# Layer 0's early fetches of the expert sums go out two per block over five blocks, and the last plan's pieces follow each other one step apart

## The chip, the cores and the metric

The kernel runs on one core of one Trainium2 chip. A time is the device time of one execution in microseconds (us), and lower is better. Times are medians over timed executions; the profile comes from one more execution, which has its own time. TensorE (PE) does matmuls, VectorE (DVE) and ScalarE (ACT) elementwise work, GpSimd (POOL) elementwise work and the indirect DMAs, SyncE (SP) only issues DMAs.

## What is computed

Two layers work on 2708 rows of 256 floats. Each layer adds to `x` first an attention over the rows that a 2708 x 2708 matrix `adj` allows, and then a mixture of experts (8 experts of width 1024 in layer 0, 16 of width 512 in layer 1), where each row goes to the two experts that its gate prefers. Cut from the reference:

```python
x = x + _L0_gnn_ref(_layernorm(x), adj, L0_gnn_W, L0_gnn_a)
x = x + _L0_ffn_ref(_layernorm(x)[None], Wg, bg, W1, b1, W2, b2)[0]
x = x + _L1_gnn_ref(_layernorm(x), adj, 1, W_gcn, W_att, a_att)
x = x + _L1_ffn_ref(_layernorm(x)[None], gate_w, gate_b, w1, b1, w2, b2, gamma, beta)[0]

# _L0_ffn_ref, the part that the change lies in
top_w, top_i = jax.lax.top_k(xf @ Wg + bg, 2)
top_w = jax.nn.softmax(top_w, axis=-1)
for e in range(E):
    h = jax.nn.gelu(xf @ W1[e] + b1[e], approximate=False)
    out = out + w_dense[:, e:e + 1] * (h @ W2[e] + b2[e])
```

## The kernel before

The rows lie in 22 tiles of 128 (two at the end are shorter), taken in 11 pairs. Layer 0's attention runs pair by pair. When a pair's attention is closed (`close0`, L1357), its rows are normalized, gated, ranked by expert and scattered by GpSimd into a table in device memory, `rows_d`, that is cut into blocks of 128 rows, each block of one expert. Layer 0's experts then run over 47 blocks in `Experts.run` (L1191), and with them layer 1 begins: its first step is to read the sums and to project them.

**One block.** For block b, TensorE does 32 matmuls for the hidden layer (L972), 2 for the turn of the next block's rows (L515), and then 1 + 16 matmuls for the outputs of block b - 1 (L987, L990). ScalarE evicts the hidden layer in eight pieces (L976, `ht`) and the turned rows (L957, `xt`). VectorE scales the outputs (L996, `yo`), and GpSimd adds them with an indirect DMA into one of two arrays in device memory, `sums0[0]` for even and `sums0[1]` for odd blocks (L1001). An add waits until the add before it on the same array has landed.

**What SyncE issues.** Its program for block b is: the first weights of block b + 2 (L834, 1 MB), the second weights of block b + 2 (L838, 1 MB, after the outputs of block b - 1, whose room they take), the rows of block b + 3 (L850, 130 KB), and then what `beside(b)` adds. Weights have three rooms. SyncE's queue is in order, so that a DMA stands behind all that were issued ahead of it.

**The early fetches.** `beside` is `combine` (L1584), which calls `ahead(b)` (L1556). Tokens of the first five pairs have all their expert rows in blocks below `DONE` = 32, so their sums are final long before the last block. In block 40 (`left == 6`), `ahead` fetches the sums of pairs 0 to 2, and in block 41 those of pairs 3 and 4: for each pair one DMA of 256 KB from each of the two arrays (`fetch_rows`, L1523 and L1528) into two places of `h_all`. Right behind a pair's fetches, GpSimd adds the two (L1566, 128x512). In blocks 43 and 44 (`left` 3 and 2) VectorE takes statistics of these rows, and in block 45 they are normalized and stored. After the last block, layer 1 goes on with these five pairs, and fetches the other six (`prepare1`, L1635).

**The plan.** Before blocks can run, the kernel must know which expert and which rows each one has. `plan` (L862) computes that with small instructions that go from VectorE to TensorE (`number_ps`, L908), back to VectorE (`at`, `sel`, L912 to L916), to TensorE (`where_ps`, L921), to ScalarE and VectorE (`where`, L925; `hot_f`, L933), to TensorE (`bias_ps`, L943) and to ScalarE (L948). It runs twice: 24 blocks when eight pairs are routed, the other 26 after the last pair, while the first blocks are already computed. Where its pieces stand among the other instructions is set by `Turns`: a piece yields a number of steps, and `in_steps` (L1349) yields `before` ahead of a TensorE piece and `after` behind one. `run` calls `steps(k)` at three places in a block with 2, 1 and 2 steps: after the hidden layer, after the turn, and after the outputs.

```python
for engine, *_ in piece:
    if "PE" in (engine, last):
        yield before if engine == "PE" else after
    last = engine
```

TensorE, ScalarE, VectorE and SyncE run in the order in which the program is written; GpSimd's order is the scheduler's.

Of the kernel before, what the change touches and what calls it, by code (L numbers as in the profile page):

```python
# [17 lines left out]
OP = mybir.AluOpType  # L18
# [41 lines left out]
class Mark:  # L60

    at = None
# [85 lines left out]
def kernel(  # L148
# [25 lines left out]
    nc = tc.nc  # L174

    ctx.enter_context(tc.manual_schedule(engines={ET.PE, ET.Activation, ET.DVE, ET.SP}))
    N, D = x.shape
# [9 lines left out]
    pairs = [tiles[k:k + 2] for k in range(0, T, 2)]  # L187
# [7 lines left out]
    SURE0, SURE1, KEEP, LATE, DEEP, AHEAD1 = 47, 45, 3, 12, 4, 8  # L195
# [56 lines left out]
    h_all = lasting.tile([P, T, D + 1], F32, name="h_all")  # L252
# [10 lines left out]
    def xn_tile():  # L263
        return lasting.tile([P, RW], F32, name="xn", bufs=4)

    def xr0_tile():
        return lasting.tile([P, RW], F32, name="xr", bufs=5)

    def xt_tile():
        return keep0.tile([P, D], F32, name="xt", bufs=3)  # L270
# [11 lines left out]
    def parts_of_rows(r):  # L282

        return [(0, r)] if r == P else [(0, 64), (64, r)]
# [33 lines left out]
    def filled(name, value, cols=1, dtype=F32, pool=const):  # L318
        tl = pool.tile([P, cols], dtype, name=name)
        nc.gpsimd.memset(tl, value)  # L320
        return tl
# [54 lines left out]
    def ts(a, s1, op0, s2=None, op1=None, dtype=F32):  # L376
        o = stat(a.shape[1], dtype)
        if op1 is None:
            nc.vector.tensor_scalar(o, a, s1, None, op0=op0)
        else:  # L380
            nc.vector.tensor_scalar(o, a, s1, s2, op0=op0, op1=op1)
        return o
# [23 lines left out]
    def at_once(steps):  # L406

        while True:
            try:
                next(steps)  # L410
            except StopIteration as end:
                return end.value
# [23 lines left out]
    def rsqrt(v, o=None):  # L436
        return at_once(rsqrt_steps(v, o))
# [88 lines left out]
    minus_one, half, ones_f = filled("minus_one", -1.0), filled("half", 0.5), filled("ones_f", 1.0, 96)  # L526
# [822 lines left out]
    def in_steps(piece, before, after):  # L1349

        last = "DVE"
# [5 lines that stand above are left out]
    def close0(pair, ahead, behind, last=False):  # L1357


        for i, r in pair:  # L1360
            ps = accs.pop(i)
            ri = row.tile([P, 1], F32, name="rinv")
            nc.vector.reciprocal(ri[:r], ps[:r, D:D + 1])
            nc.vector.scalar_tensor_tensor(x_all[:r, i, :], ps[:r, :D], ri[:r], x_all[:r, i, :],
                                           op0=OP.mult, op1=OP.add)
            experts0.store(i, r, x_all[:r, i, :])
            ln_f0.stats(x_all[:r, i, :], i, r)
            yield 1
        if last:
            lo, n = pair[0][0], len(pair)  # L1370
            rsqrt(ts(ln_f0.mv[:, lo:lo + n, 1], LN_EPS, OP.add), ln_f0.rstd[:, lo:lo + n])
        else:
            yield behind - 1
            ln_f0.root(pair)
            yield 1
            ln_f0.mend(pair)
        for t, r in pair:
            router0.rows[t] = xr0_tile()
            ln_f0.apply(router0.rows[t][:r, :D], x_all[:r, t, :], t, r)
            yield 1  # L1380
        yield ahead - 1
        router0.turn(pair)
        yield behind
        router0.evict(pair)
        yield ahead
        router0.gate(pair)
        yield behind
        router0.take(pair)
        at_once(router0.pick(pair, 0))
        yield 1  # L1390
        at_once(router0.pick(pair, 1))
        yield ahead
        router0.rank(pair)
        yield behind
        at_once(router0.number(pair))
        for t, r in pair:
            router0.scatter(t, r)
        if pair is pairs[FULL0]:
            yield from in_steps(experts0.plan(EARLY0), 1, behind)
        if last:  # L1400
            yield from in_steps(experts0.plan(experts0.NB), 1, behind)

    turns = Turns()
    sums0 = []

    FULL0 = 7
    EARLY0 = 2 * (FULL0 + 1) * 2 - E0
    experts0 = Experts(
        0, router0, L0_ffn_W1, L0_ffn_b1, L0_ffn_W2, AF.Gelu, sums0, ("wide", "acc", "mt"),
        lambda b: xn_tile() if b < 4 else late0.tile([P, RW], F32, name="xg", bufs=6),  # L1410
        lambda: xt_tile().rearrange("p (c n) -> p c n", n=P), w0_tile, SURE0)
# [26 lines left out]
    for step in range(START + T * len(pairs)):  # L1438
# [15 lines left out]
        if step >= START:  # L1454
            k, j = divmod(step - START, T)
# [21 lines left out]
    for last in late:  # L1477
        gather(*last)
    nc.scalar.preload_act_table_set(GELU_TABLE)
    turns.start(close0(pairs[-1], 2, 2, True))  # L1480
    turns.step()
    a0_scope.close()
# [40 lines left out]
    def fetch_rows(tl, src, group):  # L1523

        full = [t for t, r in group if r == P]
        if full:
            lo = full[0] * P
            ins = nc.sync.dma_start(tl[:, :len(full)], src[lo:lo + len(full) * P, :].rearrange(  # L1528
                "(t p) d -> p t d", p=P))
        if len(full) < len(group):  # L1530
            for lo, hi in parts_of_rows(TAIL):
                ins = nc.sync.dma_start(tl[lo:hi, len(full):], src[TF * P:W, :].rearrange(
                    "(t p) d -> p t d", p=P)[lo:hi])
        return ins
# [3 lines left out]
    def keep_rows(src, pair):  # L1538
        if pair[1][1] == P:
            lo = pair[0][0] * P  # L1540
            nc.sync.dma_start(x_d[lo:lo + 2 * P, :].rearrange("(t p) d -> p t d", p=P), src)
        else:
            for q, (t, r) in enumerate(pair):
                for lo, hi in parts_of_rows(r):
                    nc.sync.dma_start(x_d[t * P + lo:t * P + hi, :], src[lo:hi, q])
# [4 lines left out]
    AHEAD = 5  # L1550
    MOST, DONE = 4 * AHEAD + E0 - 1, EARLY0 + E0
    normed = {}
    assert AHEAD <= FULL0 + 1 and MOST <= DONE and DONE <= SURE0 - 9
    first, at2 = tiles[:2 * AHEAD], T - 2 * AHEAD

    def ahead(b):  # L1556

        left = SURE0 - 1 - b
        if left in (6, 5):
            for k in range(3) if left == 6 else range(3, AHEAD):  # L1560

                for half, at in ((0, 2 * k), (1, at2 + 2 * k)):
                    experts0.early_read(half, fetch_rows(h_all[:, at:at + 2, :D], sums0[half],
                                                         pairs[k]), DONE)
                xa = h_all[:, 2 * k:2 * k + 2, :D]
                nc.gpsimd.tensor_tensor(xa, xa, h_all[:, at2 + 2 * k:at2 + 2 * k + 2, :D], OP.add)  # L1566
        if left in (3, 2):
            for t, r in first[:6] if left == 3 else first[6:]:
                ln_a1.stats(x_all[:, t], t, r)
        if left == 1:  # L1570
            rsqrt(ts(ln_a1.mv[:, :2 * AHEAD, 1], LN_EPS, OP.add), ln_a1.rstd[:, :2 * AHEAD])
            for k, pair in enumerate(pairs[:AHEAD]):
                keep_rows(h_all[:, 2 * k:2 * k + 2, :D], pair)
                if k < AHEAD - 1:
                    normed[k] = [(xn_tile if k < 2 else xr0_tile)()[:, :D] for _ in pair]
                    for xp, (t, r) in zip(normed[k], pair):
                        ln_a1.apply(xp, x_all[:, t], t, r)

    with tc.tile_pool(name="experts0", bufs=1) as late0:
        room = late0.tile([P, 4096], F32, name="room2")  # L1580
        experts0.add_room(2, room[:, :2048], room[:, 2048:])
        l1_weights = []

        def combine(b):  # L1584
            if b == EARLY0 + 2:
                l1_weights.extend(load_combined(late0))
            if b == EARLY0 + 4:
                combine_weights(*l1_weights)
            ahead(b)

        experts0.run(late0, turns, (2, 1, 2), combine)
# [291 lines left out]
    xr_slots, taken_at, left = {}, {t: Mark() for t in range(0, T, 2)}, {part[0][0]: len(part) for part in parts1}  # L1883
# [617 lines left out]
```

## Time and profile before

| what | us |
|---|---|
| median of 3 timed runs | 1144.73 |
| lowest and highest of them | 1137.87 to 1148.16 |
| the profiled execution | 1135.28 |
| its span, first to last instruction | 1133.6 |
| TensorE busy in the span | 1038.0 (92%) |
| VectorE, ScalarE, GpSimd busy | 542.4, 576.4, 368.5 |
| mean granted TensorE clock | 0.961 |
| layer 0's experts, first hidden matmul to last output matmul | 294.5 to 660.6 |

The profile is read as follows. "L996 DVE ... `yo<-out_ps,w`" is an instruction of line 996 on VectorE that writes the tile `yo` from `out_ps` and `w`. In a timeline, the first two columns are the start in us from the span's start and the time that a run of like instructions takes together; "[1.96 <-DMA room...]" says that the engine stood idle 1.96 us before it and that the landing of that DMA ended the wait. A row of the stretches gives, for a stretch of the span, the busy time of each engine with its instructions, then the granted clock of TensorE, the share of the 16 DMA engines that was busy, and the GB/s that they moved. "SPq" lines are DMAs that SyncE issues, with the time that the issue took.

### The profile page before, as it was taken

To read this page: it belongs to the slowest core of one execution; us is meant where nothing else is said; L and a number is where in the kernel's file an instruction comes from. 1 tells how busy PE (TensorE), PEld (TensorE's weight loads), DVE (VectorE), ACT (ScalarE), POOL (GpSimd) and SP (SyncE) were. 2 spreads that over 40 slices of the span, in tenths; PEclk is the share of its full clock that TensorE was granted. 3 is DMA by queue.
4 is the path that set the end of the run, shared out by engine and by line. 5 is a ranking of instruction groups with operands and counts; after the bars stand their busy time and mean duration, and the time that the engine had idled before them with its cause. 6 is when DMAs were issued, how large, how long until landed. Compare 5 with 4: busy or idle time off the path is not lost. (4 is left out here: it accounts for less than half of the span.)

```text
span 1133.6 us, 21472 instructions
## 1 busy us (share of the span) xinstructions
PE 1038.0 (92%) x6707; PEld 921.6 (81%) x6707; DVE 542.4 (48%) x2210; ACT 576.4 (51%) x1602; POOL 368.5 (33%) x425
## 2 busy tenths in 40 slices
PE   5999999998989999999999999898985967999994
PEld 3788888887879999998999854898984856999882
DVE  7778888887421111101110347577865553122257
ACT  4866667664524444444444346545653633544454
POOL 7531112111242222112213361352534155434350
PEclk9999999999999999999999999997996788999997
DMA  9965454431889999999899959401114656785893
GB/s 289 282 248 177 137 176 152 170 95 55 306 252 283 331 323 321 325 305 319 257 312 331 356 155 279 160 1 51 53 61 130 179 138 144 162 203 105 227 292 129
DMA packets 161862, 234.38 MB, mean 207 GB/s; under 512 B 10891, under 2 KB 137798, under 8 KB 159032
## 3 DMA queue, kind: packets, MB, share of 16 engines
q1 hardware_dynamic: 143356, 209.90, 57.0%
q0 software_dynamic: 18384, 23.03, 10.6%
q8 instruction: 56, 0.92, 0.3%
q14 instruction: 66, 0.54, 0.2%
HBM read 205.54 MB, written 54.59 MB: 229 GB/s over the span
## 5 line engine op out<-in xcount | busy, mean ns | idle before, releaser
L996 DVE TENSOR_SCALAR yo<-out_ps,w 128x256 f32<-128x256 f32 x89 | 43.0, 483 | 383.3 <-PE out_ps L990 376.2
L1346 PE MATMUL att_ps<-g_all,z 128*128 128x257 f32 (+3 forms) x968 | 223.6, 383 | 0.0
L1346 PEld LDWEIGHTS att_ps<-g_all,z 128*128 128x128 f32 (+3 forms) x968 | 174.9, 186 | 29.5 <-issue 2.9
L990 PE MATMUL out_ps<-room,ht 128*128 128x256 f32 x840 | 191.4, 380 | 0.0
L972 PEld LDWEIGHTS hid_ps<-xt,room 128*128 128x128 f32 x1504 | 176.9, 194 | 9.3 <-issue 3.7
L972 PE MATMUL hid_ps<-xt,room 128*128 128x128 f32 x1504 | 178.9, 278 | 5.4 <-issue 2.7
L990 PEld LDWEIGHTS out_ps<-room,ht 128*128 128x128 f32 x840 | 155.5, 191 | 20.0
L1332 ACT ACTIVATE zr<-e_bc,minus_one,g_all 128x256 f32<-128x256 f32 (+3 forms) x242 | 130.2, 591 | 44.4 <-DVE z L1335 44.3
L1772 PE MATMUL att_ps<-half,wide_mask 128*128 128x258 f32 (+1 forms) x962 | 131.3, 295 | 14.9 <-issue 8.1
L976 ACT ACTIVATE ht<-hid_ps,w_t 128x128 f32<-128x128 f32 x376 | 128.6, 364 | 30.3 <-PE hid_ps L972 11.7
L1001 POOL DMA_INDIRECT sums<-yo,xg x43 | 66.8, 1554 | 233.8 <-DVE side L964 188.5
L1772 PEld LDWEIGHTS att_ps<-half,wide_mask 128*128 128x128 f32 (+1 forms) x962 | 124.5, 198 | 19.0 <-issue 14.8
L753 POOL DMA_INDIRECT rows_d<-xr,place x88 | 91.8, 1043 | 119.7 <-DVE xr L497 66.4
L1335 DVE SCALAR_TENSOR_TENSOR z<-zr,mask_t 128x256 f32<-128x256 f32 (+3 forms) x242 | 97.8, 424 | 31.1 <-ACT zr L1332 17.4
L976 ACT ACTIVATE ht<-hid_ps,w1x 128x128 f32<-128x128 f32 x180 | 65.1, 366 | 83.5 <-PE hid_ps L972 67.5
L1001 POOL DMA_INDIRECT sums<-yo,xr x42 | 65.7, 1564 | 117.0 <-DMA sums<-yo,xr 40.6
L966 ACT ACTIVATE w<-xg,side 128x1 f32<-128x1 f32 x43 | 12.7, 294 | 165.8 <-DVE side L964 165.8
L1620 POOL CAST wide_mask<-mask_t 128x1408 fp32r<-128x1408 fp8e4 x34 | 47.0, 1387 | 95.8 <-PE att_ps L1772 95.8
L972 PE MATMUL hid_ps<-lo,wide_mask 128*128 128x128 f32 x368 | 51.2, 297 | 3.5 <-ACT lo L1108 3.0
L972 PEld LDWEIGHTS hid_ps<-lo,wide_mask 128*128 128x128 f32 x368 | 49.5, 211 | 5.7 <-ACT lo L1108 3.9
L515 PE MATMUL tr_ps<-ident,xr 128*128 128x128 f32 (+1 forms) x214 | 39.6, 297 | 14.6 <-ACT xr L506 12.9
L515 PEld LDWEIGHTS tr_ps<-ident,xr 128*128 128x128 f32 (+1 forms) x214 | 28.1, 154 | 22.1 <-ACT xr L506 14.2
(334 smaller groups left out, 1442.6 us busy)
## 6 DMA issues: line engine op xcount, KB each, us to landing
room<-in_L_ffn_W_dram SPq DMA_DIRECT2D x94, 1024.0 KB
room<-in_adj_dram SPq DMA_DIRECT2D x20, 1354.0 KB
wide_mask<-in_L_ffn_w_dram SPq DMA_DIRECT2D x46, 512.0 KB
room<-in_L_ffn_w_dram SPq DMA_DIRECT2D x22, 512.0 KB
mask_t<-in_L_ffn_w_dram SPq DMA_DIRECT2D x22, 512.0 KB
rows_d<-nobody SPq DMA_DIRECT2D x1, 7511.0 KB
rows_d<-nobody SPq DMA_DIRECT2D x5, 1295.0 KB
sums<-nobody SPq DMA_DIRECT2D x2, 2944.0 KB
```

The lines of the kernel that those rows point to most:

```text
L515: nc.tensor.transpose(ps[:, c, :r], src[:, c * P:(c + 1) * P], ident[:r, :r])
L753: ins = nc.gpsimd.indirect_dma_start(out=self.rows_d[:, :], in_=self.rows[t][:r], in_offset=None, out_offset=bass.IndirectOffsetOnAxis(ap= ...
L972: nc.tensor.matmul(ps[:, :P], w1_b[:, c, f * P:(f + 1) * P], xt[:, c, :], start=(c == 0), stop=(c == DC - 1))
L976: nc.scalar.activation(ht[:, f, :], ps[:, :P], self.func, bias=self.bias[:, f, b:b + 1])
L990: nc.tensor.matmul(ps[:, :D], ht[:, f, :], self.rooms[b % self.deep][1][:, f, :], start=False, stop=(f == self.FC - 1))
L996: nc.vector.tensor_scalar(yo, ps[:, :D], w, None, op0=OP.mult)
L1001: ins = nc.gpsimd.indirect_dma_start(out=self.sums[k][:, :], in_=yo, in_offset=None, out_offset=bass.IndirectOffsetOnAxis(ap=self.rows.pop ...
L1332: nc.scalar.activation(zr[:k, :n], e_bc[:k, lo:lo + n], AF.Relu, bias=minus_one[:k], scale=g_all[:k, j, D + 1:D + 2])
L1335: nc.vector.scalar_tensor_tensor(z[:k, :n], zr[:k, :n], 1.0, mask_t[:k, j // 2, lo:lo + n, j % 2], op0=OP.add, op1=OP.mult)
L1346: nc.tensor.matmul(accs[i][:r, :D + 1], z[:k, q * P:q * P + r], g_all[:k, j, :D + 1], start=(j == 0), stop=(j == LAST))
L1620: nc.gpsimd.tensor_copy(m, src)
L1772: nc.tensor.matmul(accs[i][:, :D + 2], last_masks[i][:k] if late else wide_masks[i, j % 2][:k, j // 2, :], half_k[:k, j, :], start=(j == 0 ...
```

## The change

Three things change. The last `plan` is stepped with `after` = 1 instead of 2 (`behind` is 2 for the last pair). The fetches of pair k go out in block 36 + k, for k from 0 to 4, and GpSimd's sum of pair k is written in block 37 + k, instead of all in blocks 40 and 41. The assertion that the first of these blocks lies behind the blocks whose adds are waited for is moved with it.

```diff
         if last:
-            yield from in_steps(experts0.plan(experts0.NB), 1, behind)
+            yield from in_steps(experts0.plan(experts0.NB), 1, 1)
...
-    assert AHEAD <= FULL0 + 1 and MOST <= DONE and DONE <= SURE0 - 9
+    assert AHEAD <= FULL0 + 1 and MOST <= DONE and DONE <= SURE0 - 9 - AHEAD + 1
...
         left = SURE0 - 1 - b
-        if left in (6, 5):
-            for k in range(3) if left == 6 else range(3, AHEAD):
-
-                for half, at in ((0, 2 * k), (1, at2 + 2 * k)):
-                    experts0.early_read(half, fetch_rows(h_all[:, at:at + 2, :D], sums0[half],
-                                                         pairs[k]), DONE)
-                xa = h_all[:, 2 * k:2 * k + 2, :D]
-                nc.gpsimd.tensor_tensor(xa, xa, h_all[:, at2 + 2 * k:at2 + 2 * k + 2, :D], OP.add)
+        k = 6 + AHEAD - 1 - left
+        if 0 <= k < AHEAD:
+            for half, at in ((0, 2 * k), (1, at2 + 2 * k)):
+                experts0.early_read(half, fetch_rows(h_all[:, at:at + 2, :D], sums0[half],
+                                                     pairs[k]), DONE)
+        k -= 1
+        if 0 <= k < AHEAD:
+            xa = h_all[:, 2 * k:2 * k + 2, :D]
+            nc.gpsimd.tensor_tensor(xa, xa, h_all[:, at2 + 2 * k:at2 + 2 * k + 2, :D], OP.add)
```

In the instruction order, SyncE's pairs of fetches now stand behind the rows (L850) of blocks 36 to 40. On TensorE the bias matmuls (L943) move ahead of the turn (L515) that stood before them; on VectorE `at` and `sel` (L912 to L916) move ahead of `w`, `yo` and `side` (L994, L996, L964) of the block; on ScalarE the `where` copies (L925, L927) move ahead of eight `ht` (L976), and the bias copy (L948) ahead of the turn's copy (L957). On GpSimd the five sums stand between the last adds, one per block. Nothing else moves.

## Prediction

> **What bounds the kernel now.** I read the page from the top, then the granted clock and busy time by stretches, then TensorE's and SyncE's timelines around the two places that the diff touches.
>
> ```profile
> span 1133.6 us, 21472 instructions
> PE 1038.0 (92%) x6707; PEld 921.6 (81%) x6707; DVE 542.4 (48%) x2210; ACT 576.4 (51%) x1602; POOL 368.5 (33%) x425
> ...
> DMA 9%; DVE 1%; issue 1%; ACT 0%; SPq 0%; POOL 0%; POOLq 0%; ACTq 0%
> ```
>
> TensorE is busy 92% of the span. The chain of work that ended last reaches back only to 990 us, into layer 1, so it says nothing of layer 0; what layer 0's experts (295 to 661 us) are bound by must be read from their own stretch:
>
> ```profile
> core 0: us, PE busy (x) PEld busy (x) DVE busy (x) ACT busy (x) POOL busy (x), PEclk, DMA share, GB/s
> 400.00:500.00 100.00, 100.00 (x699) 94.27 (x698) 10.07 (x41) 44.34 (x140) 21.71 (x14) 1.00 1.00 321
> 616.00:646.00 30.00, 27.78 (x187) 25.84 (x186) 7.78 (x32) 12.60 (x38) 13.15 (x10) 0.94 1.08 363
> ```
>
> In 400 to 500 us TensorE never rests, but the DMA engines are full too: 321 GB/s at a share of 1.00. Two limits stand side by side. In 616 to 646 us, where the fetches of the sums go out, the DMA moves 363 GB/s with work always queued, and now TensorE waits:
>
> ```profile
> 608.66 3.73 PE L972 MATMUL hid_ps<-xt,room 128*128 128x128 f32 x32
> ...
> 616.01 3.73 PE L972 MATMUL hid_ps<-xt,room 128*128 128x128 f32 x32
> ...
> 625.49 5.44 PE L972 MATMUL hid_ps<-xt,room 128*128 128x128 f32 x32 [1.96 <-DMA room<-in_L_ffn_W_dram]
> ...
> 634.98 3.81 PE L972 MATMUL hid_ps<-xt,room 128*128 128x128 f32 x32 [0.27 <-DMA room<-in_L_ffn_W_dram]
> ```
>
> ```profile
> 610.47 4.97 SPq L1528 DMA_DIRECT2D h_all<-sums  x6
> 616.97 0.38 SPq L834 DMA_DIRECT2D room<-in_L_ffn_W_dram  x1
> ...
> 621.54 3.81 SPq L1528 DMA_DIRECT2D h_all<-sums  x4
> ```
>
> A block takes 616.01 - 608.66 = 7.35 us. Block 43 should have begun at 623.37; it began at 625.49, because its first weights were issued behind six fetches. Block 45 should have begun at 616.01 + 3 x 7.355 = 638.08; the timeline has it at 642.41. The two bunches make TensorE 4.33 us late.
>
> The plan is the other place. TensorE waits twice for its steps:
>
> ```profile
> 329.63 0.37 PE L921 MATMUL where_ps<-sel,owner 50*128 50x26 f32 x2 [1.17 <-DVE sel L914]
> ...
> 334.95 1.95 PE L943 MATMUL bias_ps<-hot_f,w1x 8*128 8x26 f32 x16 [0.74 <-ACT xt L957]
> ```
>
> **Part 1, the fetches.** Nothing is added or removed: ten fetches of 256 KB (0.262 MB each), five sums on GpSimd. They move from blocks 40 and 41 (six and four fetches) to blocks 36 to 40 (two each), the sums one block behind. I cost them as a queue. A steady block brings 321 GB/s x 7.355 us = 2.36 MB; with work queued the DMA moves 363 GB/s, so that takes 6.50 us and 0.85 us a block is left over. A fetch costs 0.262 / 0.363 = 0.72 us. Before: six put the queue 4.33 - 0.85 = 3.48 us behind, four another 2.89 - 0.85 = 2.04, together 5.52. TensorE was first 2.12 us late, so the loads had a lead of 3.48 - 2.12 = 1.36 us; 5.52 - 1.36 = 4.16 stands against the 4.33 read off, and the model holds to 0.2 us. The half clock in block 43 (5.44 us instead of 3.73) is then inside the 4.33: the weights would have held TensorE as long. After: two fetches cost 1.44 us, 0.59 a block more than is left over; after five blocks 2.97, less the lead 1.36, so TensorE is about 1.6 us late, in stalls of 0.41, 0.59 and 0.59 us on blocks 41 to 43. The gain is the room of three more blocks, 3 x 0.85 = 2.6 us (estimate from these rows).
>
> Here a rule of the Trainium skill speaks against the change: "DMA: Bandwidth & Descriptors", Specifications, gives the HBM share of one core as about 358 GB/s, so spreading makes no bandwidth and only spare time counts. The row shows 363, a little above. By the page a block takes 6.59 us and leaves 0.76: the gain would be 2.3 us; by the row it is 2.6, which I take. The bounds: 0 if queued transfers find no spare time, 4.33 if all stalls go. A loss is not excluded: if a stall is followed by a half clock once the wire no longer covers it, it costs 5.44 - 3.73 = 1.71 us. "TensorE: Matmul & The Clock Gate", Why this matters for your kernels, warns of idle gaps over about 3 us; the row is stricter, since 1.96 us was enough here, while the 1.17 us at 329.63 was followed by full clock. By the page no stall before or after would trip the clock and the gain is the same 2.6 us; by the row stalls of 0.6 us are also safe, and one of nearly 2 us would not be.
>
> What queues behind: on SyncE the next first-layer weights (L834) stand behind two fetches, each holding SyncE 4.97 / 6 = 0.83 us, so 1.66 us a block; without fetches SyncE sits some 3.6 us at L838 in every block, waiting for TensorE's output matmuls, and that covers it. The fetches wait for adds of blocks below 32, at least four blocks old. On GpSimd each sum (1.28 us) stands ahead of the next block's add and waits for its fetch, at worst 3.03 us so far (630.23); GpSimd idles about 5.8 us a block there (602 to 617), so the add is not late. Were that cover gone, an add would be late by what 1.28 + 3.03 = 4.31 us exceeds it. VectorE's statistics in blocks 43 and 44 find their sums two blocks older than before. Taken: 0 for each.
>
> **Part 2, the plan's steps.** Each piece of the last plan that follows a matmul now comes one step after it instead of two. Five steps make a block, and in the new order `at` and `sel` (L912, L914) stand on VectorE ahead of the block's `w`, `yo`, `side`, the two `where` copies on ScalarE ahead of eight `ht`, and the bias matmuls ahead of the turn.
>
> ```profile
> 328.50 0.48 DVE L996 TENSOR_SCALAR yo<-out_ps,w 128x256 f32<-128x256 f32 x1 [8.53 <-PE out_ps L990]
> ...
> 329.02 0.14 DVE L912 TENSOR_SCALAR at<-number_ps 50x1 f32<-50x1 f32 x1
> 329.19 0.28 DVE L914 SCALAR_TENSOR_TENSOR sel<-block_no,at,fresh 50x26 f32<-50x26 f32 x1
> ...
> 334.30 0.23 ACT L925 CAST where<-where_ps 1x26 int32<-1x26 f32 x2
> ```
>
> Before, `sel` was queued behind `yo`, which waited 8.53 us for the output matmuls, although its own input (L908, 323.32) was ready 5 us earlier. Moved ahead, it ends near 324.2 and the `where` matmuls follow the output matmuls at once: 1.17 us. The `where` copies stood behind eight `ht` (3.43 us) and freed the bank for the bias matmuls at 334.9; moved ahead they end near 329.8, `hot_f` follows, and the bias matmuls, wanted near 332.7, do not wait: 0.74 us. What is late next: `ht` starts behind two copies and `used` (0.31 us), against a first matmul group that ends at about the same time, with four banks between; taken as 0, at worst 0.3. The turn now follows the bias matmuls by 1.95 us, with 3.6 us of output matmuls to cover its copy. The first weights used here are issued 19 us ahead (321.18 for 340.40), so the DMA doesn't take the gain back. Part 2: 1.9 us, between -0.3 and 1.9.
>
> **The sum.** 2.6 + 1.9 = 4.5 us. In 661 to 707 us TensorE is the engine that goes on (43.2 of 46 us busy) and starts from the last output matmul, so the saving is passed on whole. The profiled execution, 1133.6 us of span and 1135.28 us in all, becomes 1129.1 and 1130.8. It was the fastest: the three timed runs have a median of 1144.73, 9.45 us more, for reasons that one profile can't show. I take the 4.5 us off the median: 1140.2 us, 0.4% less. About 1% (11 us) is what a measurement of this kernel can tell from no change.
>
> **The rivals.** *The wire decides* (0.20): the queued rate gives no spare time and TensorE ends as late as before, only the plan pays: 1.9 us, 1142.8. For it: the DMA share of 1.00 already in the steady stretch; against it: 363 over 321 GB/s. *The stalls vanish* (0.17): the lead is longer than 1.36 us for small bunches, all 4.33 us come back: 6.2 us, 1138.5. For it: 1.36 is inferred from one large bunch; against: the fit of 4.16 to 4.33. *The clock is dealt anew* (0.18, the slower side): in layer 1 the trace has half clock in 861 to 892, 923 to 933 and 943 to 950 us, where TensorE has idle gaps up to 8.5 us. The trace's clock changes only at whole multiples of 3.41 us from each other (625.9, 861.4, 922.9, 943.4 us); that these windows run free of the kernel no run here shows, "TensorE: Matmul & The Clock Gate" of the Trainium skill states it (What's actually happening). Moved by 4.5 us against them, the same gaps can cost more windows, each 3.41 us at half clock, hence 1.7 us of work. From three more on (5.1 us) it decides; four give 1144.7 - 4.5 + 6.8 = 1147.0. For it: the timed runs differ by 10 us; against: it can as well give windows back, and TensorE idles half of 861 to 892. That the change does nothing is excluded in its order: both moves are seen in the instruction order, and no wait holds the fetches back.
>
> **How the numbers follow.** The forecast's mechanism gets 0.45. Around the cases' times, 1138.5 to 1147, I put the scatter of the timed runs, 5 us either way, with more room below since the profiled execution lies 9.45 us under the median: 1130 to 1149. Faster by over 1% means under 1133.3: the likeliest or third case with a lucky clock, 0.10. Slower by over 1%, above 1156.2, needs the slower case's four windows and six more, or scatter in their place: 0.06. The rest is 0.84.
>
> **What would show it.** TensorE's timeline should have no wait before `where_ps` and `bias_ps`; five pairs of L1528 issues 7.4 us apart; waits for `room` under 1 us each, on blocks 41 to 43, none followed by half clock; the last output matmuls about 4.5 us earlier than 660.6; 661 to 707 unchanged in length. Wrong: a wait of 2 us for `room`, a GpSimd add that waits for `h_all`, or a layer-0 end that comes earlier with a total that doesn't.

## The result, and the profile after

| | median us | executions | ratio to before, 95% interval |
|---|---|---|---|
| before | 1144.65 | 20 | |
| changed | 1137.40 | 20 | 0.9943 [0.9925, 0.9961] |

The change gains 7.25 us in the medians, and between 4.5 and 8.6 us by the interval. The forecast was 4.5 us and 1140.2: it stands at the lower edge of the interval.

The profiled execution of the changed kernel is not shorter than that of before. Its page begins:

```profile
span 1136.1 us, 21474 instructions
PE 1039.2 (91%) x6707; PEld 922.6 (81%) x6707; DVE 545.7 (48%) x2210; ACT 577.9 (51%) x1602; POOL 368.7 (32%) x425
```

It is 2.5 us longer, so the two spans can't be subtracted; what the change did must be read in its own two places. Here are TensorE's hidden matmuls around the fetches, and SyncE's queue, in the changed kernel (start and time in us, in brackets the idle time ahead and what ended it):

```profile
611.48 3.73 PE L972 MATMUL hid_ps<-xt,room 128*128 128x128 f32 x32
...
619.50 3.81 PE L972 MATMUL hid_ps<-xt,room 128*128 128x128 f32 x32 [0.48 <-DMA room<-in_L_ffn_W_dram]
...
628.01 3.81 PE L972 MATMUL hid_ps<-xt,room 128*128 128x128 f32 x32 [0.80 <-DMA room<-in_L_ffn_W_dram]
...
635.44 3.73 PE L972 MATMUL hid_ps<-xt,room 128*128 128x128 f32 x32
```

```profile
583.57 0.25 SPq L850 DMA_DIRECT2D xg<-rows_d  x1
583.86 1.80 SPq L1528 DMA_DIRECT2D h_all<-sums  x2
...
591.64 1.59 SPq L1528 DMA_DIRECT2D h_all<-sums  x2
...
599.57 1.77 SPq L1528 DMA_DIRECT2D h_all<-sums  x2
...
606.68 2.69 SPq L1528 DMA_DIRECT2D h_all<-sums  x2
...
615.82 1.62 SPq L1528 DMA_DIRECT2D h_all<-sums  x2
...
621.14 3.25 SPq L850 DMA_DIRECT2D xg<-rows_d  x1
```

The five pairs go out one block apart. The hidden matmuls of blocks 42 and 43 come 0.67 and 1.15 us later than the cadence of 7.355 us, where before blocks 43 and 44 each came some 2.1 us late, and no half clock (a granted clock of 0.50) follows. The issue of a block's rows (L850) shows the queue falling behind: it takes 0.25 us ahead of the first pair and 3.25 us behind the last. The stretch in which the queue is fullest has this row (busy time and instructions of each engine, granted clock, DMA share, GB/s):

```profile
597.50:630.00 32.50, 31.22 (x217) 28.78 (x217) 3.26 (x14) 14.47 (x44) 13.35 (x10) 1.00 1.08 366
```

At the plan, TensorE's two waits are gone, and on VectorE `at` and `sel` now run ahead of `yo`:

```profile
333.31 0.40 PE L921 MATMUL where_ps<-sel,owner 50*128 50x26 f32 x2
...
337.64 1.96 PE L943 MATMUL bias_ps<-hot_f,w1x 8*128 8x26 f32 x16
```

```profile
327.90 0.15 DVE L912 TENSOR_SCALAR at<-number_ps 50x1 f32<-50x1 f32 x1 [5.53 <-PE number_ps L908]
328.09 0.24 DVE L914 SCALAR_TENSOR_TENSOR sel<-block_no,at,fresh 50x26 f32<-50x26 f32 x1
...
333.42 0.48 DVE L996 TENSOR_SCALAR yo<-out_ps,w 128x256 f32<-128x256 f32 x1 [4.84 <-PE out_ps L990]
```

Where did the profile lose what it gained? From the first hidden matmul to the last output matmul, layer 0's experts took 660.63 - 294.54 = 366.09 us before and 661.02 - 296.89 = 364.13 us after. They began 2.35 us later; block 3, ahead of the plan's pieces, lost some 2.6 us more than before, in TensorE's waits (4.03 instead of 2.69 us, of which 2.60 are for nothing that the profile shows and 1.43 for `ht`) and in a second half clock window; and layer 1 took 475.1 instead of 473.0 us. Differences of this size come and go between executions of one kernel: in the control below, the kernel of before run again, layer 0's experts begin 2.80 us later than in its first profile.

### The profile page after: what moved, and what is told of

The parts are those of the page before. It is cut to its first block, busy times and chain, and to the rows that moved or that the text cites. A ratio compares the mean times of both kernels' runs of the same rounds, so it can differ in the third digit from the quotient of the medians.

```text
span 1136.1 us, 21474 instructions
## 1 busy us (share of the span) xinstructions
PE 1039.2 (91%) x6707; PEld 922.6 (81%) x6707; DVE 545.7 (48%) x2210; ACT 577.9 (51%) x1602; POOL 368.7 (32%) x425
## 5 line engine op out<-in xcount | busy, mean ns | idle before, releaser
L996 DVE TENSOR_SCALAR yo<-out_ps,w 128x256 f32<-128x256 f32 x89 | 43.1, 484 | 384.0 <-PE out_ps L990 376.7
L976 ACT ACTIVATE ht<-hid_ps,w_t 128x128 f32<-128x128 f32 x376 | 128.7, 364 | 28.2 <-PE hid_ps L972 8.3
L976 ACT ACTIVATE ht<-hid_ps,w1x 128x128 f32<-128x128 f32 x180 | 65.0, 366 | 82.5 <-PE hid_ps L972 68.1
L515 PE MATMUL tr_ps<-ident,xr 128*128 128x128 f32 (+1 forms) x214 | 39.3, 294 | 15.3 <-ACT xr L506 13.0
L515 PEld LDWEIGHTS tr_ps<-ident,xr 128*128 128x128 f32 (+1 forms) x214 | 27.8, 152 | 22.9 <-ACT xr L506 14.3
```

Source lines behind the costliest of these rows:

```text
L515: nc.tensor.transpose(ps[:, c, :r], src[:, c * P:(c + 1) * P], ident[:r, :r])
L976: nc.scalar.activation(ht[:, f, :], ps[:, :P], self.func, bias=self.bias[:, f, b:b + 1])
L996: nc.vector.tensor_scalar(yo, ps[:, :D], w, None, op0=OP.mult)
```

## Experiments

Two readings are used throughout. *Lateness* is the start of block 46's hidden matmuls less that of block 36's, less ten blocks of 7.355 us: what the stalls cost there. The *plan's length* is the time from block 3's hidden matmuls to block 4's, and on to block 5's. The theory (A): a block leaves the DMA 0.85 us to spare, the loads have a lead of 1.36 us, and lateness is what the fetches put the queue behind, less that lead; the plan's gain is its two waits. The rivals were that the half clock at the bunch holds most of the 7.25 us (B), that it sits in the plan's half (C), that it comes from outside the two places (D), or that starting earlier is what counts (E).

**Each part alone, and the kernel before once more.** For the fetches alone the plan's line is as before; for the plan alone only that line is changed:

```diff
-            yield from in_steps(experts0.plan(experts0.NB), 1, behind)
+            yield from in_steps(experts0.plan(experts0.NB), 1, 1)
```

> Only the fetches are spread (two a block, blocks 36 to 40); the plan is stepped as before. Theory A (the DMA's spare time: 0.85 us a block with work queued, less a lead of 1.36 us): the waits for room at TensorE fall from 4.33 us of lateness to 1.6 to 2.0 us, the plan's two waits (1.17 and 0.74 us) stay, total about 2.4 us under before. Rival B (the half clock that follows the bunch costs the timed runs more than the one profile shows, so that this part holds most of the measured 7.25 us): 5 us or more under before. Rival C (the gain beyond the two visible parts is in the plan's half): no more than 2.4 us here, and about 5 us in the other half.

Ratio 0.9970 [0.9951, 0.9988], lateness 2.74 us, above the expected 1.6 to 2.0, the plan's waits still there. TensorE's first wait for room, on block 41, is 1.51 us, over the 1 us that the prediction allowed; the clock stayed full behind it:

```profile
610.24 3.81 PE L972 MATMUL hid_ps<-xt,room 128*128 128x128 f32 x32 [1.51 <-DMA room<-in_L_ffn_W_dram]
```

B asked for 5 us or more; the interval, 1.4 to 5.6 us, does not quite shut it out.

> The fetches alone again. Theory A with the clock's share: 2.5 to 3.5 us under before, ratio 0.997, lateness in blocks 36 to 46 of 1.5 to 2.8 us, the plan's waits of 1.17 and 0.74 us still there. Rival B: 5 us or more.

Ratio 0.9980 [0.9961, 0.9999], lateness 0.99 us, below the expected band. The interval, 0.1 to 4.4 us, shuts B out. The waits at the plan of the fetches alone, then the same lines of the plan alone:

```profile
329.62 0.37 PE L921 MATMUL where_ps<-sel,owner 50*128 50x26 f32 x2 [1.17 <-DVE sel L914]
...
334.94 1.95 PE L943 MATMUL bias_ps<-hot_f,w1x 8*128 8x26 f32 x16 [0.74 <-ACT xt L957]
```

```profile
329.75 0.40 PE L921 MATMUL where_ps<-sel,owner 50*128 50x26 f32 x2
...
334.07 1.96 PE L943 MATMUL bias_ps<-hot_f,w1x 8*128 8x26 f32 x16
```

> Only the last plan is stepped one apart; the fetches go out in two bunches as before. Theory A: the waits before where_ps and bias_ps are gone (1.91 us), the 4.33 us at the bunches stay, total about 1.9 us under before. Rival B (most of the gain is in the fetches): the same 1.9 us or less. Rival C: about 5 us under before, with a visible difference between the first hidden matmul of block 3 and that of block 6 beyond the two waits.

Ratio 0.9984 [0.9964, 1.0003]: unclear by itself, and below C's 5 us in all of its interval. Lateness 3.57 us.

> The plan alone again. Theory A with the clock's share (the two waits also help to trip a half clock window behind the bias matmuls in some executions): 1.9 to 3 us under before, ratio 0.998, lateness at the bunches 3.6 us or more, no half clock between 337 and 347 us. Rival C: 5 us or more.

Ratio 0.9989 [0.9967, 1.0012]; lateness 4.22 us; no half clock between 337 and 347 us. C falls. At the bunches, too, the clock stayed full in this profile:

```profile
625.30 3.81 PE L972 MATMUL hid_ps<-xt,room 128*128 128x128 f32 x32 [1.84 <-DMA room<-in_L_ffn_W_dram]
...
634.79 3.81 PE L972 MATMUL hid_ps<-xt,room 128*128 128x128 f32 x32 [1.89 <-DMA room<-in_L_ffn_W_dram]
```

The plan's length must be compared between profiles whose block 3 is otherwise alike. In seven it has one half clock window and 2.7 us of other waits: it took 14.35, 14.33 and 14.34 us with the plan as before, 13.15, 13.13, 13.12 and 13.15 us with the new one. The other six differ in block 3 by more than the plan (the control has no half clock there and took 12.83 us; five have 3.6 to 4.1 us of other waits and took 14.30 to 17.49), so they can't be used. Block 4 took 10.24 or 10.25 us in four profiles with the old plan and 9.50 or 9.51 in all seven with the new. That is 1.20 + 0.75 = 1.95 us, against a forecast of 1.91.

> The kernel before, unchanged, for its scatter. Every theory expects a ratio of 1.00 within its interval, waits of 1.17 and 0.74 us at the plan and 4.3 us of lateness at the bunches again. If those three numbers differ by over 1 us from the first profile, differences of that size between single profiles mean nothing.

Ratio 1.0011 [0.9992, 1.0029]. The plan's waits are the same to 0.01 us, but the lateness is 6.43 us, 2.1 us more than in the first profile: by the expectation's own words, single profiles of the bunches tell no difference of that size. TensorE's hidden matmuls in the control:

```profile
625.98 3.81 PE L972 MATMUL hid_ps<-xt,room 128*128 128x128 f32 x32 [1.32 <-DMA room<-in_L_ffn_W_dram]
...
636.57 5.43 PE L972 MATMUL hid_ps<-xt,room 128*128 128x128 f32 x32 [3.00 <-DMA room<-in_L_ffn_W_dram]
...
645.63 3.73 PE L972 MATMUL hid_ps<-xt,room 128*128 128x128 f32 x32
```

Here the half clock came behind the second bunch, when no more fetches kept the weights away, and the 1.7 us (5.43 instead of 3.73) was paid in full: the next block begins 645.63 - 636.57 = 9.06 us later.

**More room between the fetches.** Two fetches in every other block from 33 to 41, sums one block behind:

```diff
+    FROM = 33
...
-        k = 6 + AHEAD - 1 - left
+        k, odd = divmod(b - FROM, 2)
         if 0 <= k < AHEAD:
...
+            if odd == 0:
...
-        k -= 1
-        if 0 <= k < AHEAD:
...
+            else:
```

> The changed kernel, with the fetches two to a block in every other block from 33 to 41, and the sums one block behind. Theory A: two fetches cost 1.44 us and two blocks leave 1.7 us, so the queue never grows by more than the lead: no wait for room in any block, 1.9 us under the changed kernel's layer 0. Rival (a lead is lost in the fetch's own block, whatever follows): waits of 0.5 us or more stay in some of the five blocks, lateness as in the changed kernel, 1.9 us.

Ratio 0.9936 [0.9922, 0.9949], and lateness 0.01 us: the cadence holds through every block that fetches.

```profile
600.58 3.73 PE L972 MATMUL hid_ps<-xt,room 128*128 128x128 f32 x32
607.94 3.73 PE L972 MATMUL hid_ps<-xt,room 128*128 128x128 f32 x32
615.29 3.73 PE L972 MATMUL hid_ps<-xt,room 128*128 128x128 f32 x32
622.65 3.73 PE L972 MATMUL hid_ps<-xt,room 128*128 128x128 f32 x32
```

> Fetches two to a block in every other block from 33 to 41, once more and beside the changed kernel. Theory A: no wait for room again, 1.9 us under the changed kernel, 6.2 us or a ratio of 0.9946 under before. Rival (the first profile without a wait was luck): waits for room of 0.5 us or more.

Ratio 0.9945 [0.9925, 0.9965], lateness 0.01 us again. The rival, that a fetch costs its own block a wait, falls, and so does another, that what delays the weights is only SyncE's own time for issuing a pair of fetches: here it is 0.8 to 1.8 us as well (every_other), and nothing stalls. In the total times of this round the 1.9 us under the changed kernel were not seen: the changed kernel beside it had a median of 1132.42 us, from six executions only, against 1136.98 here.

**Earlier, but as bunched; and all in one.** `left in (6, 5)` becomes `left in (10, 9)`, six and four fetches in blocks 36 and 37; or `left == 6` with all five pairs in block 40.

> The kernel before with the same two bunches, six and four fetches, in blocks 36 and 37 instead of 40 and 41. Theory A (what counts is how many blocks' spare time lies between the fetches): lateness in blocks 36 to 46 as before, 3.6 to 6.4 us, ratio 1.00. Rival E (the change gains because the fetches start earlier and the DMA has more blocks to catch up): lateness as in the changed kernel, about 2 us, ratio 0.998.

Ratio 0.9984 [0.9957, 1.0011], lateness 5.26 us, in the band of theory A and far from E's 2 us. The ratio fits both, so it is this one profile that speaks against E: the fetches start in the changed kernel's block 36, and the stalls stay.

> The kernel before with all ten fetches in block 40. Theory A: the queue is 7.2 - 0.85 = 6.35 us behind after that block, less the lead of 1.36: one wait of about 5 us for room, and if the half clock that follows is not covered by the wire any more, 1.7 us on top, 5 to 6.7 us of lateness; ratio about 1.001. Rival (the wire decides by bytes alone, and spare time is nothing): the same lateness as in the kernel before, 4.3 us.

Ratio 1.0028 [1.0010, 1.0046], lateness 6.68 us, at the upper end of A's 5 to 6.7. By the ratio the same bytes cost more in one heap than in two, so the bytes alone do not decide; the lateness by itself would not show it, since the control has 6.43 us with two.

```profile
622.96 3.73 PE L972 MATMUL hid_ps<-xt,room 128*128 128x128 f32 x32
...
634.31 6.41 PE L972 MATMUL hid_ps<-xt,room 128*128 128x128 f32 x32 [3.83 <-DMA room<-in_L_ffn_W_dram]
...
644.34 3.73 PE L972 MATMUL hid_ps<-xt,room 128*128 128x128 f32 x32
```

**The whole change again.**

> The changed kernel once more, beside the kernel before on this chip. Theory A (two parts, 2.5 us and 1.9 us, as the block cadence of single profiles shows them): 4.4 us under before, a ratio near 0.996. Rival D (about 3 us more come with the change from somewhere outside the two places, as the first 7.25 us suggested): 7 us under before, a ratio near 0.9935.

Ratio 0.9898 [0.9857, 0.9940], but from six executions only; on its face this spoke for D, and the interval leaves A's 0.996 out. Lateness 1.54 us.

> The changed kernel a third time, for its difference to its own halves on one chip. Theory A with the clock's share (2.6 us at the bunches, 1.9 us at the plan, and one half clock window fewer in an average run, about 1.4 us): 6 us under before, ratio 0.995. Rival D (about 3 us from somewhere else): ratio 0.9925 or lower at the same mean clock.

Ratio 0.9963 [0.9945, 0.9981] from 22 executions, 4.2 us; lateness 2.14 us. D's 0.9925 lies outside; the 6 us that A expected with the clock's share lie at the edge of the interval, so that share was not seen here. The granted clock speaks against D too. Executions of one kernel differ by 10 us and more, and their mean granted clock goes with it. A fit over all executions of the experiments and the kernel before beside them (a level for each of the two chips, one for each kernel, and one slope for the clock; one execution of 1726 us left out) gives 9.2 us for each 0.01 of mean clock and leaves a scatter of 2.0 instead of 3.4 us. At equal clock it has:

| kernel | us against before, at equal clock (2 standard errors) | without the clock | lateness in its profiles, us |
|---|---|---|---|
| changed | -4.8 (0.8) | -5.8 (1.4) | 1.90, 1.54, 2.14 |
| fetches alone | -2.5 (0.7) | -3.6 (1.2) | 2.74, 0.99 |
| plan alone | -1.9 (0.8) | -2.7 (1.4) | 3.57, 4.22 |
| every other block | -6.0 (0.9) | -6.8 (1.5) | 0.01, 0.01 |
| bunched early | -0.4 (1.3) | -1.2 (2.2) | 5.26 |
| all in one block | +1.2 (1.1) | +4.5 (1.8) | 6.68 |
| before | 0 | 0 | 4.34, 6.43 |

The halves add up to the whole, 2.5 + 1.9 = 4.4 against 4.8. Every other block is 1.2 us under the changed kernel, with 1.1 us of uncertainty. D's 7 us are shut out at equal clock, but without it the whole has 5.8 (1.4), which does not shut them out. The 1 us between these two figures rests on six executions of the changed kernel on one chip, with a mean clock of 0.961 against 0.957 before; on the other chip, with 22 executions, the clock is the same, 0.959, and the means differ by 4.4 us. So no share of the clock in the change's gain is shown, and the first 7.25 us is taken as the upper part of its scatter.

## Why the prediction was right

**Part 1, forecast 2.6 us.** Right in mechanism and size. Four profiles with the bunches (before, control, the plan alone twice) have a mean lateness of 4.64 us, five with the change's fetches 1.86: 2.8 us, although single profiles lie between 3.57 and 6.43, and between 0.99 and 2.74. The model of the queue also told the three other layouts: none in every other block, as before when bunched early, 5 to 6.7 in one heap. Bytes and an earlier start are not what was gained; the spare time of three more blocks fits all five layouts. Its 0.85 us a block stays an estimate from two rates; no run measured it by itself. The page's 358 GB/s would have given 2.3 us; the rows, 363 before and 366 after, stand a little above it, and the two sums are too near to be told apart by these runs.

**What was off in it.** The stalls came in two blocks (0.67 and 1.15 us) and not in three of 0.41, 0.59 and 0.59; in the five profiles with these fetches they begin on block 41, 42 or 43. So the lead is not the same 1.36 us every time, and why is open. The step "the half clock in block 43 is then inside the 4.33" held for that profile: the second profile of the plan alone has no half clock there, and its blocks 43 and 44 come as late, 2.00 and 2.13 us; its second wait is 1.89 us, where before it is 0.27 behind a half clock of 1.7. It does not hold always: in the control the half clock came behind the second wait and cost the whole 1.7. GpSimd's sums waited up to 3.34 us for their fetches in the changed kernel, a little over the 3.03 allowed, and the engine still stood idle ahead of every add. One sign was not met: the last output matmul came at 661.02 us, and not 4.5 us ahead of 660.6, for what was lost ahead of the plan.

**Part 2, forecast 1.9 us.** Right: 1.95 us in the profiles, 1.9 at equal clock. Nothing was late next: `ht`, the turn and the bias matmuls had no new wait, and the bound of -0.3 was not reached. What preceded the plan in block 3 moved single profiles by more than that.

**Passing it on.** 661 to 707 us was as long as before: from the last output matmul to the first attention matmul 706.91 - 660.63 = 46.28 us before and 707.29 - 661.02 = 46.27 after.

**The rivals.** "The wire decides" and "the stalls vanish" are both shut out for this change by the lateness of 1.5 to 2.1 us; the second came true only for every other block. "The clock is dealt anew", which made the changed kernel slower than before, did not show: it was faster in all three comparisons. Two of six profiles with the old plan, those of the two bunch experiments, have a half clock window right behind the bias matmuls, none of seven with the new plan; in the early bunch it looks like this, where the output matmuls take 3.62 us elsewhere:

```profile
339.70 1.95 PE L943 MATMUL bias_ps<-hot_f,w1x 8*128 8x26 f32 x16 [0.73 <-ACT xt L957]
...
341.70 5.30 PE L990 MATMUL out_ps<-room,ht 128*128 128x256 f32 x16
```

The section on the hardware shows what sets these two profiles apart. No run made such a window come or go on purpose, and why TensorE waits in block 3 for nothing that the profile shows was not tried.

## What to carry to other kernels

When TensorE and the DMA are both full, an extra transfer is paid from the spare time between the moments at which it is issued: work out what a block leaves over, and space the transfers so that each one's cost is earned before the next. Here 1.44 us of fetches and 0.85 us a block meant every other block, and that version had no stall at all: 6.0 us (0.9) under the kernel before at equal clock, and in the blocks that fetch some 1.9 us under the changed one. A small chain of steps beside the main loop does best, as here with `sel` and `yo`, ahead of the instruction that waits longest on its engine; and a change of a few us is read by the cadence of the blocks in its own stretch, not by the difference of two spans.

## What the hardware showed that was not expected

The mean granted clock goes with most of the scatter of this kernel: 9.2 us for each 0.01, which brings the scatter from 3.4 to 2.0 us.

Half clock (TensorE granted half its clock) comes and goes on a grid. In each of the 13 profiles its starts lie whole multiples of 3.41 us apart, and the grid stands elsewhere against the kernel each time: 1.27 us past the span's start (less whole multiples) in the first profile, 1.68 us in the control of the same kernel, and from 0.37 to 3.39 us over all. The prediction left open whether these windows run free of the kernel; the 13 profiles show that they do. What counts at the fetches is how long TensorE stands idle inside one stretch of this grid. In the first profile the wait of 1.96 us lies in one stretch, 1.46 us of 3.41 busy, and the next stretch has half clock; in the second profile of the plan alone the wait of 1.89 us is cut in two, 1.33 and 0.56 us idle, and the clock stays full (the first busy time of a row is TensorE's, and the granted clock stands third from its end):

```profile
622.50:625.91 3.41, 1.46 (x9) 1.02 (x8) 0.76 (x3) 0.29 (x1) 1.57 (x2) 1.00 1.09 352
625.91:629.32 3.41, 3.41 (x19) 3.41 (x18) 0.00 (x0) 1.47 (x4) 1.28 (x1) 0.50 1.10 342
```

```profile
630.81:634.22 3.41, 2.08 (x10) 1.50 (x8) 1.25 (x5) 0.29 (x1) 2.33 (x4) 1.00 1.04 391
634.22:637.64 3.42, 2.85 (x25) 2.88 (x26) 2.38 (x11) 1.81 (x5) 1.53 (x1) 1.00 1.08 383
```

In all 13 profiles, from 295 to 360 and from 575 to 660 us, every stretch at full clock with 1.94 us idle or more (16 of them) was followed by half clock. None with 1.79 us or less was, but for two: those behind the bias matmuls in the two bunch experiments. Only there do the wait of 0.73 us and all 16 bias matmuls of 8 rows (1.95 us) fall in one stretch; in the other four profiles with the old plan the grid cuts between or through them. Without the wait, the 16 matmuls in one stretch did not bring half clock (the plan alone, 334.07 to 336.03 us). The Trainium skill's "TensorE: Matmul & The Clock Gate" (What's actually happening) has a window of 3.4 us that runs free of the kernel, which these profiles bear out; its figure of about 3 us for a harmful gap (Why this matters for your kernels) is too long here.

SyncE, too, was held: issuing the rows of a block (L850), 0.25 us in steady blocks, took up to 3.25 us in the changed kernel and 3.85 us in the control, once fetches stood ahead of it. What sets that time no run shows.
